# Twelve vector operations on data that nothing reads, in front of the first statistics of a two-layer convolution kernel

## The chip, the cores and the metric

The kernel runs on one core of a Trainium2 chip. A core has a matrix engine (TensorE, PE in the profile), a vector engine (VectorE, DVE), a scalar engine (ScalarE, ACT), a general engine (GpSimd, POOL) and a queue engine that issues transfers (SyncE, SP). Each works through its own queue in order and waits on semaphores for the others. Data lie in a working memory of 128 partitions (SBUF) and in the banks that TensorE writes to (PSUM); 16 DMA engines move data between the device memory and SBUF. The metric is device time in microseconds (us) of one execution; lower is better.

## The reference

The input x has 384 channels of 192 by 192 pixels, float32. Two layers follow each other; both normalise x over 32 groups of 12 channels first (`_gn`: mean and variance over the group's channels and all its pixels) and add their result to x:

```python
x = x + L0(_gn(x), ...)   # 1x1 conv to 3*384 channels, 2x2 max pool, 3x3 depthwise conv,
                          # attention over channels in 8 heads, gelu, repeat, 1x1 conv
x = x + L1(_gn(x), w)     # 7x7 depthwise conv with a symmetrised kernel
```

Nothing of layer 0 can be finished before the group statistics of x are known, since they scale the weights of its first convolution.

## The kernel before, in words

The channels are three tiles of 128 partitions (`KT = 3`), x is cut into 24 blocks of 8 image rows (`NB = 24`, `BLK` = 1536 pixels per channel). The function `conv_preact_d2` builds everything; most of the order on each engine is left to a scheduler, and what is wrapped in `keep` (`tc.keep_in_program_order`) keeps the order in which it is written.

The part around the change, in the order of the text:

- L122 to L151: constants. `ident`, `ones`, `gsel` (which channels share a group) and others are filled by VectorE and POOL.
- L153 to L185: ACT's queue issues the loads of the weights; POOL makes the symmetrised 7x7 weights.
- L253: `vrows, rowbuf`, a buffer for image rows. The change stands right behind this line.
- L255 to L278: the pools `xpool` (three block buffers) and `parkp`; `z`, a tile of ones and zeros, is filled by VectorE (L265, L266), and the PSUM banks `grams`, `bank_x`, `bank_y` and so on are opened.
- L309 to L420: the first statistics, of channel tiles 0 and 1. Pool `xsp`, tag `xs`, has five buffers. The first is taken by `xe` (L317), an extra slice of channel tile 2; the others are cycled through by the blocks. SP issues the loads (L413); VectorE takes `bn_stats` of each 512 pixels (L337, six per block of two channel tiles; L418 for `xe`). The blocks come from the last to the first; 21 go through the five buffers, the last three (b = 2, 1, 0) into buffers of `xpool` that stay (`held`).
- L394 to L408: after 21 blocks the statistics are aggregated (L356) and TensorE sums them over the groups (L344).
- L421 to L434: the three held blocks' statistics are added, mean and reciprocal deviation come out (L377 to L383, with POOL's power), and ACT scales the weights `wq` (L434).
- L436 to L454: TensorE begins the first convolution of the held blocks (L442), ACT sets the sums aside (L448).
- L459 to L482: meanwhile the statistics of channel tile 2 are taken in the same manner (loads L477, tag `xs` again).
- L808: a matrix product on `z` opens the bank `grams`; it is early in TensorE's queue and needs no load.

After that the kernel runs through the first layer, its attention and the second layer, none of which the change touches. A few later lines serve below as examples of what an operation takes: L861 (a 32 by 32 transpose on VectorE of 384 elements per partition), L1269 (a sum over `lower` with its two dimensions swapped, so that it is read with a stride of 24 floats), L1254 (the same sum read densely), L1253 and L1117 (dense vector operations of two inputs), L1510 (an addition that moves pixels in a strided order), L929 (a multiply-add on rows of 96), L233 and L1955 (copies out of PSUM).

Of the kernel before, what the change touches and what calls it, by code (L numbers as in the profile page):

```python
# [8 lines left out]
F32 = mybir.dt.float32  # L9
AF = mybir.ActivationFunctionType  # L10
ALU = mybir.AluOpType
AX = mybir.AxisListType

P = 128
# [72 lines left out]
def conv_preact_d2(  # L87
# [17 lines left out]
    nc = tc.nc  # L105
    PSUM = bass.MemoryType.PSUM
# [17 lines left out]
    ones = const.tile([P, P], F32, name="ones")  # L124
# [119 lines left out]
    def row_tiles(pool, name, n):  # L244

        t = pool.tile([P, n * KT * ROW], F32, name=name)
        rows = [
            t[:, k * ROW : (k + 1) * ROW].rearrange("p (t c) -> p t c", c=PS + 2)
            for k in range(n * KT)
        ]  # L250
        return [rows[k : k + KT] for k in range(0, n * KT, KT)], t

    vrows, rowbuf = row_tiles(rowp, "rows", 3)  # L253

    xctx = ExitStack()  # L255
    xpool = xctx.enter_context(tc.tile_pool(name="xpool", bufs=NX))
    parkp = xctx.enter_context(tc.tile_pool(name="parkp", bufs=1))
# [51 lines left out]
    with tc.tile_pool(name="stp", bufs=1) as stp, tc.tile_pool(name="xsp", bufs=5) as xsp:  # L309
# [57 lines left out]
        def both(kt, most, mid):  # L367

            last = moments(aggregate(kt, 0, NX, "last"), mid, f"{kt}_last")
            nc.vector.scalar_tensor_tensor(most, last, NX / NB, most, ALU.mult, ALU.add)  # L370
            return most
# [107 lines left out]
        d = both(kt, dm, mid)  # L479
# [24 lines left out]
    for i in range(3):  # L504
        w = wq[:, TWO, i * C : (i + 1) * C]
# [926 lines left out]
    for i in range(3):  # L1432
        t = sxp.tile([P, LEAD + CP * RB * RUN + LEAD], F32, name=f"sx{i}")
# [582 lines left out]
```

## Time and profile before

| | us |
|---|---|
| median of 4 runs | 2700.42 (2699.68 to 2701.9) |
| the profiled execution | 2701.9 |
| its span, first to last instruction | 2700.2 |
| TensorE matmul busy | 2506.2 (93%) |
| VectorE busy | 2238.1 (83%) |
| ACT busy | 1420.3 (53%) |
| POOL busy | 1460.3 (54%) |

In the page, the busy times are of the whole span; the view in order of time gives start, length, engine, source line, operation, output and inputs with their shapes (partitions by elements), a count where equal operations follow each other, and in brackets how long the engine had been idle before and what released it. A length includes the time that an instruction overlaps the next one of its engine. "PEld" are TensorE's weight loads. A view by stretch gives, for each engine, the busy time and in brackets the number of instructions, and then the granted TensorE clock, the busy share of the DMA engines and the rate in GB/s.

### The profile page before, as it was taken

How to read it: one execution, taken by the hardware profiler on the slowest of the kernel's cores; microseconds unless marked ns; L12 is line 12 of the kernel's file. 1: busy time of each engine (PE TensorE's matmuls, PEld its weight loads, DVE VectorE, ACT ScalarE, POOL GpSimd, SP SyncE). 2: the span in 40 equal slices, each digit the busy share in tenths (PEclk: the TensorE clock that was granted, in tenths of full speed). 3: DMA queues.
4: the chain of work that ended last, by engine and by line, in shares of the span. 5: the costliest groups of instructions: out<-in, count | busy, mean ns of one | idle time of the engine just before them, and what ended most of it. 6: DMA issues, size and time to landing. Idle time of an engine off the chain costs nothing. (4 is left out here: it accounts for less than half of the span.)

```text
span 2700.2 us, 29574 instructions
## 1 busy us (share of the span) xinstructions
PE 2506.2 (93%) x8893; PEld 1630.7 (60%) x8893; DVE 2238.1 (83%) x3172; ACT 1420.3 (53%) x2711; POOL 1460.3 (54%) x1587
## 2 busy tenths in 40 slices
PE   0298999999999999999899989999999799999998
PEld 0144566656666656665556656666666577777776
DVE  7986788888888888877799969998888789886876
ACT  0032667676767676776212223223234677777776
POOL 1013788888887988875213311001011677777877
PEclk9999999999999999999999989999999899999999
DMA  9962354445453635443429996757657999999998
GB/s 378 400 242 53 109 172 125 148 128 177 118 183 87 190 110 188 112 115 72 141 96 335 373 317 221 241 178 251 211 162 254 328 345 362 368 368 369 371 372 259
DMA packets 467630, 609.59 MB, mean 226 GB/s; under 512 B 250224, under 2 KB 399312, under 8 KB 450704
## 3 DMA queue, kind: packets, MB, share of 16 engines
q1 hardware_dynamic: 407104, 311.83, 36.9%
q0 software_dynamic: 37344, 148.84, 15.5%
q10 hardware_dynamic: 23024, 147.05, 14.6%
q8 instruction: 71, 1.16, 0.2%
q14 instruction: 87, 0.71, 0.1%
HBM read 370.93 MB, written 208.21 MB: 214 GB/s over the span
## 5 line engine op out<-in xcount | busy, mean ns | idle before, releaser
L563 PE MATMUL pv<-xv,wq 128*128 128x384 f32 x1512 | 499.8, 492 | 21.9 <-DMA xv<-in_x_dram 11.0
L1920 PE MATMUL pc<-main,w 128*128 128x288 f32 x1536 | 435.2, 406 | 3.9 <-POOL aux L1848 1.9
L563 PEld LDWEIGHTS pv<-xv,wq 128*128 128x128 f32 x1512 | 290.5, 193 | 222.8 <-issue 10.8
L1940 DVE TENSOR_SCALAR apart<-pc,rb 32x576 f32<-32x576 f32 x384 | 312.2, 813 | 107.3 <-PE pc L1920 98.1
L897 POOL TENSOR_TENSOR qk<-qk,more 128x384 f32<-128x384 f32 x290 | 309.5, 1073 | 110.3 <-ACT more L896 101.4
L1938 ACT ACTIVATE apart<-pc,rb 32x576 f32<-32x576 f32 x384 | 281.0, 732 | 132.5 <-PE pc L1920 127.7
L1551 POOL DMA_DIRECT2D sd<-sx x96 | 72.4, 758 | 506.4 <-DVE sx L1510 487.8
L1920 PEld LDWEIGHTS pc<-main,w 128*128 128x128 f32 x1536 | 290.1, 189 | 87.7 <-PE pc L1920 3.4
L596 DVE SCALAR_TENSOR_TENSOR vb<-rows,wd,vb 128x576 f32<-128x576 f32 x360 | 293.7, 818 | 10.7
L897 POOL TENSOR_TENSOR qk<-qk,rows 128x384 f32<-128x384 f32 x216 | 230.3, 1071 | 76.3 <-ACT rows L896 70.1
L1920 PE MATMUL pc<-aux,h 128*128 128x288 f32 x768 | 248.8, 406 | 0.4 <-POOL main L1828 0.2
L1879 POOL COPY res<-apart 128x1152 f32<-128x1152 f32 (+1 forms) x96 | 218.9, 2311 | 55.0 <-DMA out_dram<-res 42.7
L929 DVE SCALAR_TENSOR_TENSOR bank_r<-ring,wd,bank_r 128x384 f32<-128x384 f32 x383 | 236.3, 617 | 6.9
L1037 PE MATMUL bank_b<-rows,more 128*128 128x384 f32 x528 | 220.6, 500 | 1.9 <-ACT bank_c L1139 1.0
L1510 DVE TENSOR_TENSOR sx<-xr,y 128x576 f32<-128x576 f32 x180 | 203.8, 1173 | 18.8 <-ACT y L1481 15.1
L569 DVE TENSOR_REDUCE rows<-pv 128x192 f32<-128x768 f32 x144 | 137.7, 956 | 59.4 <-PE pv L563 59.3
L1530 ACT ACTIVATE wq<-sx,negmid 128x1152 f32<-128x1152 f32 x96 | 120.6, 1256 | 118.8 <-DVE sx L1510 116.6
L1117 DVE TENSOR_TENSOR rows<-bank_c,rows 128x384 f32<-128x384 f32 x132 | 73.3, 555 | 127.2 <-PE bank_c L1037 68.9
L1920 PEld LDWEIGHTS pc<-aux,h 128*128 128x128 f32 x768 | 144.9, 189 | 43.0 <-POOL main L1828 2.5
L896 ACT ACTIVATE more<-ring,wd 128x384 f32<-128x384 f32 x290 | 170.3, 609 | 0.0
L1456 ACT ACTIVATE gl<-po 128x288 f32<-128x288 f32 x96 | 39.4, 410 | 221.4 <-PE po L1449 221.4
L1037 PE MATMUL bank_x<-xq,wq 128*128 128x384 f32 x378 | 154.8, 491 | 1.0 <-ACT bank_b L1089 1.0
(349 smaller groups left out, 4922.9 us busy)
## 6 DMA issues: line engine op xcount, KB each, us to landing
sd<-sx POOLq DMA_DIRECT2D x96, 600.0 KB, 10.1
out_dram<-res SPq DMA_DIRECT2D x192, 288.0 KB, 11.2
main<-sd ACTq DMA_DIRECT2D x46, 1200.0 KB, 6.6
xr<-in_x_dram SPq DMA_DIRECT2D x45, 1152.0 KB, 12.6
xq<-in_x_dram SPq DMA_DIRECT2D x21, 2304.0 KB, 8.6
xv<-in_x_dram SPq DMA_DIRECT2D x126, 384.0 KB, 8.0
w<-wt ACTq DMA_DIRECT2D x46, 1024.0 KB, 7.5
xs<-in_x_dram SPq DMA_DIRECT2D x24, 1536.0 KB, 15.2
```

What stands on the lines that cost most here:

```text
L563: nc.tensor.matmul(ps[:, u, 0 : RB * HW], wq[:, kt, o : o + P], xb[:, u, kt, :], start=(kt == 0), stop=(kt == KT - 1),)
L569: nc.vector.tensor_reduce(rows[ct][:, 1 + t0 : 1 + t0 + UT, 1 : PS + 1], ps[:, :, 0 : RB * HW].rearrange("p u (a w b) -> p u w a b", a=2, ...
L596: pin(nc.vector.scalar_tensor_tensor(dst, src, w, dst, ALU.mult, ALU.add))
L896: keep(nc.scalar.mul(part.rearrange("p (h w) -> p h w", w=PS), src, w))
L897: keep(nc.gpsimd.tensor_tensor(flat, flat, part, ALU.add))
L929: nc.vector.scalar_tensor_tensor(into, src, w, before, ALU.mult, ALU.add)
L1037: nc.tensor.matmul(ps[:, 0:HN], lhs, rhs, start=start, stop=True, skip_group_check=True)
L1510: nc.vector.tensor_tensor(bass.AP(flat.tensor, flat.offset + at(e) + a * RUN, [flat.ap[0], [JP, NT], [1, NJ], [at(f) - at(e), 2]],), xq[:, ...
L1879: keep(copy(res[ps, k], apart[ps, :, k].rearrange("p e n -> p n e")))
L1920: nc.tensor.matmul(ahead[q][:, k, 0 : NT * NJ], lhs, rhs, start=(j == 0), stop=(j == 2), skip_group_check=True,)
L1938: keep(nc.scalar.mul(dst, src, scale))
L1940: keep(nc.vector.tensor_scalar_mul(dst, src, scale))
```

## The change

Two SBUF tiles of 6144 floats per partition (`tin`, `tout`) and two PSUM banks (`bank`) are opened for a while and closed again before `xpool` opens. VectorE fills all three with ones, does seven transposes of 768 elements per partition with different strides, an addition of 256 elements with strides and one scaled copy of 288 elements out of PSUM; ACT does two more of these copies. Nothing reads `tout` afterwards. All of it is pinned in the order of the text among itself. Since the space is used again by what is opened next, TensorE's L808 and the load of the first held block now wait for ACT's copies. Lines behind L253 move down by 34; the line numbers in the text are those of the kernel before.

```diff
     vrows, rowbuf = row_tiles(rowp, "rows", 3)
 
+    with tc.tile_pool(name="trial", bufs=1) as trial, tc.tile_pool(
+        name="trial_p", bufs=1, space=PSUM
+    ) as trial_p:
+        order_of = tc.keep_in_program_order
+        tin = trial.tile([P, 6144], F32, name="tin")
+        tout = trial.tile([P, 6144], F32, name="tout")
+        bank = trial_p.tile([P, 2, 512], F32, name="trial_b")
+        order_of(nc.vector.memset(tin, 1.0))
+        order_of(nc.vector.memset(bank, 1.0))
+        order_of(nc.vector.memset(tout, 1.0))
+
+        def v(t, *dims):
+            return bass.AP(t.tensor, t.offset, [t.ap[0], *[list(d) for d in dims]])
+
+        def w(t, o, *dims):
+            return bass.AP(t.tensor, t.offset + o, [t.ap[0], *[list(d) for d in dims]])
+
+        turn = lambda a, b: order_of(nc.vector.transpose(a, b))
+        turn(v(tout, (1, 768)), v(tin, (1, 768)))
+        turn(v(tout, (32, 24), (1, 32)), v(tin, (1, 24), (24, 32)))
+        turn(v(tout, (8, 24), (192, 4), (1, 8)), v(tin, (32, 24), (1, 32)))
+        turn(w(tout, 576, (8, 24), (-192, 4), (1, 8)), v(tin, (32, 24), (1, 32)))
+        turn(v(tout, (8, 24), (192, 4), (1, 8)), v(tin, (384, 12), (32, 2), (1, 32)))
+        turn(v(tout, (1, 24), (24, 32)), v(tin, (32, 24), (1, 32)))
+        turn(v(tout, (192, 4), (8, 24), (1, 8)), v(tin, (32, 24), (1, 32)))
+        order_of(nc.vector.tensor_tensor(
+            w(tout, 2048, (68, 2), (8, 32), (1, 4)), w(tout, 2048, (68, 2), (8, 32), (1, 4)),
+            v(tin, (32, 2), (0, 4), (1, 32)), ALU.add))
+        order_of(nc.vector.tensor_scalar_mul(
+            v(tout, (1, 2), (32, 12), (384, 12)), v(bank, (512, 2), (12, 12), (1, 12)), tin[:, 0:1]))
+        order_of(nc.scalar.mul(
+            w(tout, 1, (1, 2), (32, 12), (384, 12)), v(bank, (512, 2), (12, 12), (1, 12)), ones[:, 0:1]))
+        order_of(nc.scalar.mul(
+            w(tout, 2048, (12, 2), (24, 12), (1, 12)), v(bank, (512, 2), (12, 12), (1, 12)), ones[:, 0:1]))
     xctx = ExitStack()
```

In an access pattern each pair is a stride and a count in floats, the outermost first.

## The prediction

> **What bounds the kernel now.** I read the page first, then the order in time at the start of the run, since the change stands there.
>
> ```profile
> span 2700.2 us, 29574 instructions
> ...
> PE 2506.2 (93%) x8893; PEld 1630.7 (60%) x8893; DVE 2238.1 (83%) x3172; ACT 1420.3 (53%) x2711; POOL 1460.3 (54%) x1587
> ```
>
> TensorE carries the kernel as a whole, but it has nothing to do before the first statistics are in. VectorE in order of time (start, length, instruction, count; in brackets the idle time before it and what ended it):
>
> ```profile
> 1.46 0.48 DVE L266 MEMSET z<- 128x512 f32 x1
> 7.17 2.86 DVE L418 BATCH_NORM_STATS2 ste<-xe 128x6 f32<-128x384 f32 x6 [5.22 <-DMA xe<-in_x_dram]
> ...
> 10.41 0.15 DVE L420 TENSOR_SCALAR me<-mve 128x1 f32<-128x1 f32 x1
> 13.98 3.66 DVE L337 BATCH_NORM_STATS2 st<-xs 128x6 f32<-128x512 f32 x6 [3.42 <-DMA xs<-in_x_dram]
> 18.20 3.66 DVE L337 BATCH_NORM_STATS2 st<-xs 128x6 f32<-128x512 f32 x6 [0.56 <-DMA xs<-in_x_dram]
> 26.38 3.66 DVE L337 BATCH_NORM_STATS2 st<-xs 128x6 f32<-128x512 f32 x6 [4.52 <-DMA xs<-in_x_dram]
> 30.29 68.01 DVE L337 BATCH_NORM_STATS2 st<-xs 128x6 f32<-128x512 f32 x108 [0.25 <-DMA xs<-in_x_dram]
> 98.22 3.56 DVE L356 BATCH_NORM_AGGREGATE mv_most<-st 128x2 f32<-128x378 f32 x2
> ...
> 105.56 10.77 DVE L337 BATCH_NORM_STATS2 st<-xs 128x6 f32<-128x512 f32 x18
> ...
> 120.42 37.47 DVE L337 BATCH_NORM_STATS2 st<-xt 128x6 f32<-128x512 f32 x63
> ```
>
> Two things are to be seen. First, idle time until 26.38: VectorE starts waiting at 1.95 and waits for loads in four pieces, 5.22 + 3.42 + 0.56 + 4.52 = 13.7 us. Second, a small reserve in the long stretch: 108 statistics take 98.22 - 30.29 = 67.93 us, 0.629 each, while 18 of them on data long landed take (10.77 - 0.68) / 17 = 0.594 each. So from 30.29 on a block of six comes every 3.77 us, where VectorE alone needs 3.58; the loads set that pace. 18 blocks hold 67.93 - 18 x 3.58 = 3.5 us that a late VectorE can win back. After 98.22 it can win back nothing: the 18 and the 63 run at 0.594, without waits.
>
> That stretch releases TensorE (all engines in order of time, then a stretch by engine):
>
> ```profile
> 120.45 1.12 POOL L382 TENSOR_TENSOR rstd<-rstd,halfneg 128x1 f32<-128x1 f32 x2 [88.48 <-DVE mean L383]
> 121.07 2.77 ACT L434 ACTIVATE wq<-wq,rstd 128x768 f32<-128x768 f32 x4 [100.57 <-POOL rstd L382]
> 122.06 6.30 PE L442 MATMUL bank_b<-xs,wq 128*128 128x512 f32 x8 [2.16 <-ACT wq L434]
> ...
> 140.00:160.00 20.00, 20.00 (x48) 8.80 (x47) 20.00 (x33) 7.02 (x12) 0.00 (x0) 1.00 0.95 357
> ```
>
> From 122 TensorE is full (20.00 of 20.00 us) and VectorE too, so what is late at 98.22 ends the kernel that much later.
>
> **The prices.** From the views by tile and by line (shortest, middle and longest ns; start; shape):
>
> ```profile
> L265 DVE MEMSET z<- x1: 308/308/308, 1.1 to 1.1; 128x300 f32 x1
> L266 DVE MEMSET z<- x1: 485/485/485, 1.5 to 1.5; 128x512 f32 x1
> ...
> L861 DVE STREAM_TRANSPOSE turns<-qk x144: 534/578/579, 203.3 to 1297.3; 128x384 f32<-128x384 f32 x144
> ...
> L1269 DVE TENSOR_REDUCE after<-lower x1: 1575/1575/1575, 1322.2 to 1322.2; 128x24 f32<-128x576 f32 x1
> ...
> L1254 DVE TENSOR_REDUCE seconds<-sq x3: 753/753/754, 1325.7 to 1352.1; 128x24 f32<-128x576 f32 x3
> ```
>
> - Memset: 177 ns for 212 elements, 0.835 ns each; 6144 elements are 5.13 us from start to start. Two of them: 10.26.
> - Memset of the two PSUM banks, 1024 elements: no row has one. Below, the same slope, 0.86 us; above, the slope of VectorE's copies out of PSUM (L1955 282 ns for 128, L233 558 for 384: 1.08 ns), 1.10. I take 0.95, nearer to the memset rows.
> - Dense transpose of 768: 578 + 384 x 1.04 (the slope of the statistics, 543 ns for 384, 676 for 512) = 978 ns; the statistics start 83 ns before their predecessor's recorded end (676 long, 593 apart), so 0.89 from start to start. Four more of the seven are like it for VectorE: the third to fifth write runs of 8, the seventh's pattern folds into a contiguous one. No row has runs of 8 in a store, so their upper bound is the next price.
> - The second transpose reads with a stride of 24 floats. L1269 reduces along the same stride, L1254 the same shape densely: 822 ns more for 576 elements, 1.43 ns each, 1.10 us for 768. So 1.99. The sixth stores with that stride: between nothing more and the same 1.10, middle 0.55, so 1.44; no row speaks for either end.
> - The strided sum of 256: L1253 takes 458 ns for 288 densely, so 0.35 apart. The scaled copy of 288 out of PSUM: 0.38 by the copies above, up to 0.41 more for scattered stores; I take 0.58.
>
> Memset against a rule: the Trainium skill, "VectorE: DVE Perf Modes", section "Zero memsets can be issued as uint32 (trn2)", says that a memset takes one cycle per element whatever its type, and the same page gives VectorE 0.96 GHz. That is 6.40 us for 6144, against 5.13 by the rows; by the rule both memsets would cost 2.5 us more and the forecast would be 2704.8. The rows are of the same instruction on the same memory, so I go by them.
>
> **The change, step by step.** In the built program VectorE's queue has 12 new operations, ACT's two; the order on all engines is otherwise the old one but for one thing: the new operations are interleaved with the first xs block's statistics, and xe's six statistics stand behind them. VectorE after:
> - 1.10 + 5.13 + 0.95 + 5.13 = 12.31; z 0.26, first transpose 0.89, z 0.43, second 1.99: 15.88. The first xs block (landed at 13.98) waits 1.9 us.
> - Its six statistics 3.58; transposes three, four, five and seven 3.56; the sixth 1.44; the sum 0.35; the copy 0.58: 25.39. The transposes wait for one another's end, but a statistic stands between each two, which covers the wait; without it each would lose its 0.08 of overlap, 0.4 in all.
> - xe's statistics 6 x 0.463 = 2.78: 28.17. Second block 3.58 and the small ones 0.40: 32.15. Third block: 35.73.
>
> The fourth block began at 30.29, so VectorE is 5.4 us late there. Of the 20.0 us of new work, 14.6 disappear in the old waits: the 13.7 above, 0.25 at 30.29 and small gaps. 18 blocks win back 3.5; 1.9 are left at 98.22 and reach the end.
>
> Loads: tag xs has five buffers, xe holds one. The fifth xs load waits for xe's statistics and goes out at 28.2 instead of 19.7; the third and fourth are then still in flight (landing at 26.38 and 30.29), and xe's own load took 6.3 us from issue to landing, so it lands by 34.5 instead of 34.06, where VectorE wants it only at 39.3. Later loads are issued up to 5.4 us later of a lead whose middle was 15.2. Were that cover gone, each late load would cost what it lands late.
>
> Costs at nothing: ACT's two copies (under 1 us each at about 26) end in its idle stretch of 100.57 us; ACT's queue only needs to be free at 121. The first matmul of TensorE (L808) now waits for ACT's reading of the bank, 2.0 becomes about 27; behind it in the queue stands L344 at 100.2. The held loads wait for ACT too, but go out at 79.8. POOL's queue is unchanged.
>
> Sum: the profiled execution took 2701.9 (1.7 around the span), 1.5 over the median of the four runs; 2701.9 + 1.9 = 2703.8 for it, and from the median 2700.4 **2702.3**.
>
> **The rivals.**
> - *All hidden.* If strides cost nothing (1.10, 0.55 and 0.20 less), 1.9 shrinks to 0.1: 2700.5. For it: the loads set the pace until 98. Against: L1269.
> - *Slower.* Stores in runs of 8 are scattered for VectorE too: transposes three to five cost 1.99 each, the sixth too. 3 x 1.10 + 0.55 = 3.85 more, 5.8 in all, 2706.2. It decides from 2.0 us per transpose on. For it: L1510, which moves pairs with strides, takes 1174 ns for 576 where dense L1253 takes 757. Against: runs of 96 cost little (L929 617 ns for 384, dense L1117 558), and 8 lies between 2 and 96.
> - *Faster.* No wait is removed; only another order of loads could do it.
> - *The work isn't done*, since nothing reads it: then 2700.4. Against it, all twelve operations stand in VectorE's queue. 0.00.
>
> **How the numbers follow.** 0.2% (5.4 us) is about what a measurement of this kernel can tell from no change. Likeliest case 0.60, own range 2700.9 to 2703.8 (sixth transpose, copy and bank at their ends: 0.9 more or 0.8 less; the scatter of the runs: 0.6). All hidden 0.22. In between 0.05: the three transposes with runs of 8 dearer than dense, but not by 1.10 each. Slower 0.11: runs of 8 dear. Faster 0.02. The first three stay within 0.2%: 0.87. The range takes in the hidden case with the scatter of the runs (2699.7 to 2701.9) and reaches to the edge of the slower one: 2699.8 to 2706.0.
>
> **What would show it.** Right: memsets of about 5.1 us, the first block's statistics between 16 and 25, no waits for loads between 26 and 90, the aggregates at about 100.1, TensorE's L442 at about 124. Wrong: transposes three to five near 2 us; or L442 still at 122; or waits for loads behind a late VectorE, which would mean that the late releases starve the queue; or a gap that opens after 122.

## The result, and the profile after

| | us |
|---|---|
| before, median of 76 runs | 2701.28 (2694.54 to 2711.72) |
| after, median of 51 runs | 2706.89 (2696.9 to 2720.32) |
| ratio after / before, 95% interval | 1.0018 (1.0012 to 1.0025) |
| the profiled execution after (span) | 2704.29 (2702.6) |

The ratio is estimated from the runs and is not the quotient of the two medians, which would be 1.0021 (5.6 us). By the ratio the change costs 4.9 us (3.2 to 6.8). The forecast was 2702.3 from a median of 2700.42, so 1.9 us; the measured time lies 0.9 us above the range. Line numbers of the kernel after are 34 higher from L254 on.

The first two lines of the page after:

```profile
span 2702.6 us, 29590 instructions
...
PE 2507.0 (93%) x8893; PEld 1632.7 (60%) x8893; DVE 2260.3 (84%) x3184; ACT 1421.3 (53%) x2713; POOL 1465.2 (54%) x1587
```

VectorE has twelve instructions more (3184 against 3172) and 22.2 us more of busy time; the span of this one execution is only 2.4 us longer. Where most of the work went is seen in VectorE's order of time at the start (start, length, instruction, count; in brackets the idle time before and what ended it):

```profile
2.32 5.18 DVE L262 MEMSET tin<- 128x6144 f32 x1 [1.23 <-issue]
7.71 0.91 DVE L263 MEMSET trial_b<- 128x1024 f32 x1 [0.21 <-issue]
9.89 5.18 DVE L264 MEMSET tout<- 128x6144 f32 x1 [1.27 <-issue]
15.08 0.31 DVE L299 MEMSET z<- 128x300 f32 x1
15.42 0.98 DVE L272 STREAM_TRANSPOSE tout<-tin 128x768 f32<-128x768 f32 x1
...
16.86 1.89 DVE L272 STREAM_TRANSPOSE tout<-tin 128x768 f32<-128x768 f32 x1
18.68 0.65 DVE L371 BATCH_NORM_STATS2 st<-xs 128x6 f32<-128x512 f32 x1
19.26 0.95 DVE L272 STREAM_TRANSPOSE tout<-tin 128x768 f32<-128x768 f32 x1
...
23.61 2.06 DVE L272 STREAM_TRANSPOSE tout<-tin 128x768 f32<-128x768 f32 x1
...
28.45 2.83 DVE L452 BATCH_NORM_STATS2 ste<-xe 128x6 f32<-128x384 f32 x6
...
38.55 3.65 DVE L371 BATCH_NORM_STATS2 st<-xs 128x6 f32<-128x512 f32 x6
...
89.57 13.14 DVE L371 BATCH_NORM_STATS2 st<-xs 128x6 f32<-128x512 f32 x22
102.63 3.56 DVE L390 BATCH_NORM_AGGREGATE mv_most<-st 128x2 f32<-128x378 f32 x2
```

The row at 38.55 is the fourth block (30.29 before). Every wait for a load is gone, as expected. But the memsets do not lie end to end in their rows: 1.23, 0.21 and 1.27 us of "issue" stand ahead of them. From the end of one to the end of the next, the last one takes 9.89 + 5.18 - (7.71 + 0.91) = 6.45 us, not 5.13. The view of VectorE's waits between 0 and 95 us (what waited, for what; us in total, times, longest) has nothing else left:

```profile
DVE tout L264 <- issue: 1.3, 1, 1.3
DVE tin L262 <- issue: 1.2, 1, 1.2
DVE ones L125 <- PEq L2035: 0.9, 1, 0.9
DVE trial_b L263 <- issue: 0.2, 1, 0.2
```

A stretch of the kernel after (length; busy time and instructions of PE, PEld, DVE, ACT, POOL; granted clock, busy share of the DMA engines, GB/s) shows the paced part:

```profile
32.00:100.00 68.00, 0.00 (x0) 0.00 (x0) 68.00 (x117) 0.00 (x0) 0.17 (x1) 1.00 1.01 413
```

VectorE is busy for 68.00 of 68.00 us and is itself the bound now; the loads still run at 413 GB/s. And the release of TensorE, all engines in order of time:

```profile
124.87 1.12 POOL L416 TENSOR_TENSOR rstd<-rstd,halfneg 128x1 f32<-128x1 f32 x2 [92.70 <-DVE mean L417]
125.49 2.77 ACT L468 ACTIVATE wq<-wq,rstd 128x768 f32<-128x768 f32 x4 [95.57 <-POOL rstd L416]
126.47 2.93 PE L476 MATMUL bank_b<-xs,wq 128*128 128x512 f32 x3 [2.16 <-ACT wq L468]
```

The aggregate starts at 102.63 instead of 98.22, TensorE's first matmul of the layer (L442, now L476) at 126.47 instead of 122.06: 4.41 us late both times, with nothing lost or won between.

The two profiled executions alone do not show these 4.41 us at the end. Compared matmul by matmul, the kernel after is 3.9 us behind at 1300 us, 3.1 at 1900, 0.4 at 2500, and its span ends 2.4 us later. Single executions wander by several us there (see the part on the scatter), so what arrives at the end is read from the many runs: 4.9 us, with 4.4 inside the interval.

So the account by the two traces is: VectorE got 23.0 us of new work (14.0 for the memsets end to end, 9.0 for the rest from start to start); 18.6 of them went into waits and into the reserve of the paced blocks, and 4.4 came out at the aggregate.

### The profile page after: what moved, and what is told of

It is laid out like the page before. It is cut to its first block, busy times and chain, and to the rows that moved or that the text cites. A ratio compares the mean times of both kernels' runs of the same rounds, so it can differ in the third digit from the quotient of the medians.

```text
span 2702.6 us, 29590 instructions
## 1 busy us (share of the span) xinstructions
PE 2507.0 (93%) x8893; PEld 1632.7 (60%) x8893; DVE 2260.3 (84%) x3184; ACT 1421.3 (53%) x2713; POOL 1465.2 (54%) x1587
## 4 chain that ended last, share of the span: by engine, by line
PE 73%; DMA 13%; DVE 9%; POOL 2%; issue 2%; SPq 1%; ACT 1%; POOLq 0%; DVEq 0%; ACTq 0%
PE pv L597 19%; DMA out_dram<-res 11%; PE bank_b L1071 9%; PE pc L1954 7%; PE bank_y L1071 6%; PE bank_d L1071 6%; PE bank_c L1071 6%; PE bank_x L1071 6%; PE pr L1507 4%; DVE st L371 3%; PE po L1483 3%; PE grams L830 2%; DVE sx L1544 1%; POOL res L1913 1%; DVE vb L630 1%
```

## The experiments

Two theories were set against each other. **Theory A**: the twelve operations are work in front of a stage with a fixed amount of cover; what exceeds the cover comes out at the aggregate and reaches the end one to one, and the memsets, at 1.04 ns per element, are why it is 4.4 and not 1.9. **The rivals**: the loss is in proportion to the work, or it has a price of its own that cover does not touch (late loads, the pinned order, the waits of TensorE and ACT). All kernels of one group ran on the same chip beside the kernel before.

### Short memsets, and the memsets alone

The first run keeps the change and fills only what the later operations read (768 + 640 elements of `tin` and 384 of `tout`; the expectation says 1536 for the first two):

```diff
-        order_of(nc.vector.memset(tin, 1.0))
+        order_of(nc.vector.memset(tin[:, 0:768], 1.0))
+        order_of(nc.vector.memset(tin[:, 768:4608].rearrange("p (n c) -> p n c", c=384)[:, :, 0:64], 1.0))
         order_of(nc.vector.memset(bank, 1.0))
-        order_of(nc.vector.memset(tout, 1.0))
+        order_of(nc.vector.memset(tout[:, 2048:2432], 1.0))
```

> Theory A: the changed kernel loses its time because VectorE is 4.4 us late at the first aggregate, and half of that lateness is the memsets, which hold VectorE 1.042 ns per element (end to end 6.41 us for 6144) although their rows are 0.835 ns per element long. Here only the elements that are read are filled (1536 and 384 in place of twice 6144), everything else of the change stays. By A VectorE has 24.1 us of work before the third block, which lands at 26.4, so it is not late: aggregate at 98.2 to 98.5, ratio to the kernel before 1.000. Rival B: the loss comes from the strided transposes, the PSUM copies or the waits for ACT; then most of the 1.0018 stays, aggregate later than 101.

The second keeps the three memsets of the change and drops what follows them (the transposes, the sum and the three copies):

```diff
         order_of(nc.vector.memset(bank, 1.0))
         order_of(nc.vector.memset(tout, 1.0))
-        turn = lambda a, b: order_of(nc.vector.transpose(a, b))
-        ...
```

> Only the three memsets of the change, without transposes, sum and copies. Theory A: the memsets end at 15.1, z at 15.9, first block, extra slice and second block at 26.3; the third block lands at 26.4, so VectorE is in time: aggregate at 98.2 to 98.6, ratio 1.000. Together with the run with short memsets this says that each half is free and only both together cost 4.4 us. Rival C: what is added in front costs about in proportion to its length, memsets 13.9 of 22.8 us: 2.7 us, ratio 1.001, aggregate at about 101.

Measured: the short memsets took 2710.96 us against 2711.27 of the kernel before, ratio 1.0005 (0.9994 to 1.0016); the memsets alone 2712.68, ratio 1.0004 (0.9992 to 1.0016). The aggregates start at 98.33 and 98.20 us (98.22 before). VectorE in order of time, with the short memsets:

```profile
14.08 0.69 DVE L372 BATCH_NORM_STATS2 st<-xs 128x6 f32<-128x512 f32 x1 [0.35 <-DMA xs<-in_x_dram]
...
26.50 3.66 DVE L372 BATCH_NORM_STATS2 st<-xs 128x6 f32<-128x512 f32 x6 [1.75 <-DMA xs<-in_x_dram]
30.41 30.13 DVE L372 BATCH_NORM_STATS2 st<-xs 128x6 f32<-128x512 f32 x48 [0.25 <-DMA xs<-in_x_dram]
...
98.33 3.56 DVE L391 BATCH_NORM_AGGREGATE mv_most<-st 128x2 f32<-128x378 f32 x2
```

and with the memsets alone:

```profile
26.34 3.66 DVE L348 BATCH_NORM_STATS2 st<-xs 128x6 f32<-128x512 f32 x6 [0.17 <-DMA xs<-in_x_dram]
30.26 30.14 DVE L348 BATCH_NORM_STATS2 st<-xs 128x6 f32<-128x512 f32 x48 [0.27 <-DMA xs<-in_x_dram]
...
98.20 3.56 DVE L367 BATCH_NORM_AGGREGATE mv_most<-st 128x2 f32<-128x378 f32 x2
```

Each half still waits for the third and fourth block, so each is wholly hidden: 0.1 and 0.0 us at the aggregate. Together they cost 4.41. At the aggregate the loss isn't in proportion to the work, and it isn't a price of the transposes, of the pinned order or of the waits for ACT, which the first of the two runs keeps; it is what is left when the cover is used up. The end times could not have told this: both intervals reach to 1.0016, which is 4.3 us.

### More of the same work

```diff
         order_of(nc.vector.memset(tout, 1.0))
+        for t in (tin, tout, tin, tout):
+            order_of(nc.vector.memset(t, 1.0))
```

> The changed kernel with four more memsets of 6144. Nothing covers them any more, so by theory A (6.41 us each) the aggregate comes 25.6 us later than in the changed kernel, at 128.3, and the time is 4.4 + 25.6 = 30.0 us over the kernel before, ratio 1.0111. If the rows' length (5.18 us) were what they cost and the 1.25 us in front of each a delay of the first instructions alone: 20.7 more, aggregate at 123.3, 25.1 us over before, ratio 1.0093. If the later part of the kernel gave lateness back, as the end of the changed kernel's profile looks like, less than the aggregate's shift would arrive at the end.

Measured: 2742.9 us against 2711.27, ratio 1.0121 (1.01 to 1.0142), that is 32.8 us (27.1 to 38.5). The aggregate starts at 128.26, TensorE's first matmul 30.03 us later than before. The memsets in order of time:

```profile
9.89 5.18 DVE L264 MEMSET tout<- 128x6144 f32 x1 [1.27 <-issue]
16.30 5.18 DVE L266 MEMSET tin<- 128x6144 f32 x1 [1.23 <-issue]
22.70 5.18 DVE L266 MEMSET tout<- 128x6144 f32 x1 [1.23 <-issue]
...
128.26 1.84 DVE L392 BATCH_NORM_AGGREGATE mv_most<-st 128x2 f32<-128x378 f32 x1
```

They start 6.41 us apart, and 4.41 + 4 x 6.41 = 30.05. With the cover gone, each memset comes out in full, at 6.41 and not at its row's 5.18, and the kernel's end follows: 30.0 lies inside the interval of the 32.8. This is the run that decides the price of a memset: with the rows' price the aggregate would stand at 123.3.

### A sweep of sizes and strides

Memsets of 768 to 6144 elements, and transposes of 768 elements with load strides 1, 2, 3, 4, 8, store strides 2, 3, 4, 8 and stores in runs of 2 and 4, in place of what the change does after its first two memsets:

```diff
+        for n in (768, 1536, 3072, 6144):
+            order_of(nc.vector.memset(tout[:, 0:n], 1.0))
+        turn = lambda a, b: order_of(nc.vector.transpose(a, b))
+        dense = lambda t: v(t, (32, 24), (1, 32))
+        for k in (1, 2, 3, 4, 8):
+            turn(dense(tout), v(tin, (32 * k, 24), (k, 32)))
+        for k in (2, 3, 4, 8):
+            turn(v(tout, (32 * k, 24), (k, 32)), dense(tin))
+        for k in (2, 4):
+            turn(v(tout, (k, 24), (192, 32 // k), (1, k)), dense(tin))
```

> Prices by themselves: memsets of 6144, 1024 (PSUM), 768, 1536, 3072 and 6144, then transposes of 768 whose loads have strides of 1, 2, 3, 4 and 8 floats, whose stores have strides of 2, 3, 4 and 8, and whose stores come in runs of 2 and 4. Theory A: each memset holds VectorE 1.042 ns per element whatever its size, in rows of 0.70, 1.34, 2.62 and 5.18 us. Transposes: if what counts is how many neighbours lie in the same 16 bytes (the Trainium skill, SBUF - State Buffer, on cachelines), strides of 2 and runs of 2 cost the dense 0.95 us, strides of 4 and 8 the 1.9 us that stride 24 took, 3 in between. If the distance counts, cost grows with the stride and 2 already costs more. The whole is some 11 us more work than the change's: aggregate at 112 to 116.

Measured in one execution: the aggregate starts at 111.20 us, a little under what was expected. VectorE in order of time; the transposes shown are load strides 3, 4 and 8, then store strides 4 and 8 and runs of 4:

```profile
12.52 2.62 DVE L265 MEMSET tout<- 128x3072 f32 x1 [0.59 <-DVE z L289]
...
17.10 5.18 DVE L265 MEMSET tout<- 128x6144 f32 x1 [1.23 <-issue]
...
25.64 1.19 DVE L270 STREAM_TRANSPOSE tout<-tin 128x768 f32<-128x768 f32 x1
...
27.31 1.53 DVE L270 STREAM_TRANSPOSE tout<-tin 128x768 f32<-128x768 f32 x1
...
29.32 1.55 DVE L270 STREAM_TRANSPOSE tout<-tin 128x768 f32<-128x768 f32 x1
...
34.03 1.51 DVE L270 STREAM_TRANSPOSE tout<-tin 128x768 f32<-128x768 f32 x1
...
35.80 1.55 DVE L270 STREAM_TRANSPOSE tout<-tin 128x768 f32<-128x768 f32 x1
...
38.92 0.97 DVE L270 STREAM_TRANSPOSE tout<-tin 128x768 f32<-128x768 f32 x1
```

The rows of the memsets grow by (5.18 - 2.62) / 3072 = 0.833 ns per element, and the idle time ahead of them grows too, by (1.23 - 0.59) / 3072 = 0.208 ns; together 1.041 ns. So a fifth of a memset is booked as a gap in front of its row (the 0.59 is even put down to another memset, `z`). Of the transposes, stride 2 costs nothing in a load (0.956 us), 3 costs 0.24 us more than dense, 4 and 8 cost 0.58 and 0.60, stores nearly the same, and runs of 2 and 4 in the store are dense (0.967 and 0.970). So 2 is free and 3 lies between, as expected, but 4 and 8 take 1.5 us and not the 1.9 of stride 24.

### The change once more, and the loads in another order

If the cover is made of waits for loads, taking waits out of the kernel before must make the change dearer. A part of the waits was put down to `wq` (1728 KB, L162), which ACT's queue sends for at the very start, ahead of most of the blocks. A first attempt moves that load behind ACT's small loads, without and with the change; the change itself ran beside them.

```diff
-    nc.scalar.dma_start(wq, wqkvT.rearrange("(t p) o -> p t o", p=P))
     nc.scalar.dma_start(bq, bqkv)
     ...
+    nc.scalar.dma_start(wq, wqkvT.rearrange("(t p) o -> p t o", p=P))
```

> The kernel before with one move: the load of wq (1.7 MB) is issued behind ACT's small loads instead of ahead of them. In the kernel before SP's third xs load waits 11.2 us for the small load bp, which stands behind wq, and the DMA engines run at 126 and 187 GB/s from 16 to 22. Theory A says that what the first aggregate gains the end gains: third block 4 us earlier, aggregate at 94 to 95, L442 at 118, ratio 0.9985. Rival: wq's bytes only come later among the blocks, the aggregate stays at 98, ratio 1.000.

> The change and the move of wq together. By theory A the changed kernel has VectorE busy from 1.1 to 102.6 without a wait for a load, so earlier loads can't help it: aggregate again at 102.6, L442 at 126.5, ratio to the kernel before 1.0016; the price of the change against the kernel with small loads first is then 8 us and not 4.4. If the price were that of the work itself, the aggregate would come at about 98.5.

> The changed kernel once more, beside the two below on one chip. Theory A: TensorE's first product on x (L442) at 126.5 instead of 122.1, 4.4 us, and the ratio near 1.0016; what differs from that in one execution comes from TensorE's wait for loads between 1550 and 1610, which was 11 us in the profile of before, 25 in that with the memsets alone.

Measured against 2713.11 us of the kernel before on that chip: 2712.39 with the load moved, ratio 0.9995 (0.9983 to 1.0006); 2714.23 with the change on top, 1.0002 (0.9992 to 1.0012); the change alone 2716.18, 1.0011 (1.0 to 1.0023). The aggregates start at 98.50, 102.62 and 102.63. VectorE in order of time, with the load moved:

```profile
14.44 3.66 DVE L337 BATCH_NORM_STATS2 st<-xs 128x6 f32<-128x512 f32 x6 [4.85 <-DMA xs<-in_x_dram]
...
23.54 3.66 DVE L337 BATCH_NORM_STATS2 st<-xs 128x6 f32<-128x512 f32 x6 [1.45 <-DMA xs<-in_x_dram]
30.36 3.66 DVE L337 BATCH_NORM_STATS2 st<-xs 128x6 f32<-128x512 f32 x6 [3.16 <-DMA xs<-in_x_dram]
```

The attempt missed its aim: the waits only moved from the third block to the fourth, since `wq` still travels ahead of the aggregate, and the first block's load now goes out at 6.2 us instead of 1.3. The kernel without the change got no faster, so these runs can't tell a price of cover from a price of its own. What they repeat is the change's 4.1 and 4.4 us at the aggregate. At the end, the run with both misses its expectation: 1.0016 lies above its interval, although its first matmul (L476) starts at 126.46, as late as with the change alone. Where its profile loses the lateness again stands in the part on the scatter.

The second attempt takes `wq` out of the stage: SP sends for it behind the last held block.

```diff
-    nc.scalar.dma_start(wq, wqkvT.rearrange("(t p) o -> p t o", p=P))
...
             nc.sync.dma_start(xb, xv[:, 0:TWO, b * BLK : (b + 1) * BLK])
+            if b == 0:
+                nc.sync.dma_start(wq, wqkvT.rearrange("(t p) o -> p t o", p=P))
```

> The kernel before, with wq's load (1.7 MB, needed by ACT only at 121) taken out of ACT's queue and issued by SP behind the last held block. The run with the small loads first gained nothing because wq's bytes still went out ahead of the first aggregate and the first block's load was issued 4.9 us later. Here 4.2 us of transfer (1.77 MB at 417 GB/s) leave the stretch ahead of the aggregate: first block at about 11.5, one block each 3.77, aggregate at 90 to 93, L442 at 114 to 117. Theory A (what is gained at the aggregate reaches the end): 5 to 8 us, ratio 0.997 to 0.998. Rival: the loads that follow or a later stage take it back, ratio 1.000 although the aggregate is early.

> The same with the change. Theory A: VectorE works from 1.1 on without a wait for a load, so its aggregate stays at 102.6 and L442 at 126.5; the same twelve operations then cost 10 to 12 us against the kernel with wq behind the blocks, where they cost 4.4 against the kernel before. Ratio to the kernel before 1.0016, and 1.004 to the kernel with wq behind the blocks. If the work had a price of its own, the aggregate would come 4.4 us behind that of the other run, at 95 to 97.

Measured against 2711.48 us: without the change 2707.79, ratio 0.9991 (0.9979 to 1.0002); with it 2717.64, ratio 1.0021 (1.0009 to 1.0034). VectorE in order of time without the change:

```profile
18.63 3.66 DVE L336 BATCH_NORM_STATS2 st<-xs 128x6 f32<-128x512 f32 x6 [0.32 <-DMA xs<-in_x_dram]
22.59 37.72 DVE L336 BATCH_NORM_STATS2 st<-xs 128x6 f32<-128x512 f32 x60 [0.30 <-DMA xs<-in_x_dram]
...
94.34 3.56 DVE L355 BATCH_NORM_AGGREGATE mv_most<-st 128x2 f32<-128x378 f32 x2
```

and with it:

```profile
102.61 3.59 DVE L389 BATCH_NORM_AGGREGATE mv_most<-st 128x2 f32<-128x378 f32 x2
```

Without the change the 4.52 us wait is gone and the aggregate starts 3.88 us earlier (less than the 5 to 8 expected; 1728 KB at the 416 GB/s of that stage are 4.25 us, about what was won). With the change the aggregate stands at 102.61, where it stands without the moved load too. The twelve operations now cost 102.61 - 94.34 = 8.27 us against the kernel that has `wq` late, and (1.0021 - 0.9991) x 2711.5 = 8.1 us at the end. The two profiled executions, on one chip, are 8.31 us apart at TensorE's first matmul (118.18 and 126.49) and 8.5 us in their spans (2704.4 and 2712.9), so here the lateness can be followed to the end. But the pair is not as clean as it was meant to be: with the change the scheduler let SP send for `wq` at 8.8 us already (77.5 without the change), so its bytes were in the stage after all, and a price of its own of 4.4 us on the old supply would give 102.6 as well. What speaks in this run is that VectorE had no wait for a load up to 95 us, so that no other supply could have helped it; the case against a price of its own rests on the two halves that cost nothing.

Without the change this last kernel has the lowest ratio of all, with a median 3.7 us under the kernel before, but its interval just reaches 1, so a gain is likely and not shown.

### Where the scatter of the runs sits

The medians of the kernel before differ by chip (2701 in the first runs, 2711 to 2713 in those of the experiments). In the profiles one stretch of the second layer carries much of such differences, at about 1560 us, where TensorE waits for the load of `xv`. The columns are those of the stretches above; the kernel before in its first profile:

```profile
1560.00:1575.00 15.00, 4.12 (x6) 1.56 (x7) 3.66 (x4) 4.42 (x10) 6.33 (x9) 0.64 1.04 368
```

and the kernel with the memsets alone:

```profile
1560.00:1575.00 15.00, 0.00 (x0) 0.00 (x0) 4.48 (x4) 3.18 (x7) 5.08 (x7) 0.62 1.03 374
```

TensorE's longest wait there was 5.3 us in the first and 18.6 us in the second (all its waits there 11.0 and 23.2 us; the expectation above has 25). The changed kernel had 5.1 us in its first profile and 17.5 us when run again on another chip; it was 18.7 with `wq` behind the blocks and the change. The DMA engines are full in all of them (1.03, 1.04). So it goes with the chip or the execution, not with the edit. What makes the one stretch short and the other long was not followed up.

A second such stretch is at about 1330 us. With the change and the small loads first, TensorE is 4.3 us behind the kernel before at 1300 us, matmul by matmul, and 1.1 us at 1334; in between, its idle time ahead of a matmul on `xv` is 2.72 us, against 4.50 in the change run again, and its clock was granted in full (first the change run again, then the small loads first with the change):

```profile
1325.00:1340.00 15.00, 10.50 (x28) 5.65 (x27) 12.90 (x18) 4.50 (x18) 1.10 (x2) 0.89 0.87 290
1325.00:1340.00 15.00, 12.28 (x38) 6.87 (x37) 14.03 (x19) 4.50 (x18) 0.59 (x1) 1.00 0.86 289
```

This is one execution, and whether the moved loads or chance did it stays open.

## Why the prediction was wrong, point by point

**The mechanism held.** VectorE's late start was to be covered by its four waits first, then by the reserve of the paced blocks, and what was left was to reach the end one to one. The first two are shown, and the third as far as TensorE's first matmul: no wait for a load is left up to 95 us, the blocks won back 38.55 - 30.29 = 8.26 down to 4.41, 3.85 against the 3.5 forecast, and the 4.41 stand unchanged there. At the end the ratios of the change (4.9 us, 3.2 to 6.8) and of the four memsets more (32.8 us, 27.1 to 38.5) agree with it; the run with the small loads first and the change does not. The runs with half the work and with four memsets more moved the aggregate as this says (0 and 30 us).

**The step that failed is the price of the memsets**: "Memset: 177 ns for 212 elements, 0.835 ns each; 6144 elements are 5.13 us from start to start". 0.835 is the slope of the row's length, and it was taken for the spacing of the rows. Measured, each of the two takes 6.41 to 6.45 us end to end, 1.04 ns per element, and the one on PSUM 1.12, just over its upper bound of 1.10: together 2.8 us more. The prediction's own sign, "memsets of about 5.1 us", came true in the rows (5.18) and said nothing of the price; "the aggregates at about 100.1" and "TensorE's L442 at about 124" showed it wrong (102.63 and 126.47). The same two rows of the kernel before would have told it, read by their ends: 1.46 + 0.48 = 1.94 and 1.10 + 0.31 = 1.41 lie 0.53 apart, and the first ends some 0.33 after its predecessor (1.02 + 0.06 = 1.08), so 0.20 to 0.22 for 212 elements, about 1 ns each. The page's two decimals blur it (the raw times give 0.541 - 0.320 = 0.221, 1.04 ns), but not down to 0.835.

**The rule weighed was right.** The Trainium skill, "VectorE: DVE Perf Modes", section "Zero memsets can be issued as uint32 (trn2)", gives one cycle per element. With the page's 0.96 GHz that is an estimate of 1.042 ns; measured 1.041. The prediction said what the sum would be by it, 2704.8, and 2700.4 + 4.41 is 2704.8. That the two agree to a tenth is partly luck: VectorE came to the fourth block 0.3 us later than by that sum, and the paced blocks won back 0.35 more than forecast. "The rows are of the same instruction on the same memory, so I go by them" was true of the rows and wrong of how they were read: a row that disagrees with a rule by a fifth calls for a second reading of the same trace, by the ends, before it is preferred.

**The smaller terms**, from start to start: the sixth transpose 1.85 against 1.44, so a store with a stride of 24 floats lies nearer to its upper bound of 1.99 than to the middle that was taken (+0.41); the second 1.82 against 1.99; the dense ones 0.88 against 0.89; the sum 0.31 against 0.35; the copy out of PSUM 0.55 against 0.58. The statistics of `xe` and the two blocks behind them took 0.2 less. All in all VectorE reached the fourth block at 38.55 instead of 35.73, 2.82 late, of which the memsets are 2.77.

**The rivals.** *Slower* by dear stores in runs of 8 fell: transposes three to five have rows of 0.95 like the dense ones (0.98). *All hidden* fell, since strides of 24 do cost (1.89 and 2.06). *Costs at nothing* held for ACT (two copies, 0.75 and 0.50 us, at 28.6 and 29.4), for L808 (30.0 instead of 2.0, the next thing in its queue far behind) and for the loads, since nobody waits for one. But they went otherwise than forecast: the fifth goes out at 27.9 when the first block's statistics end, not those of `xe`, and the next four go out 8 to 13 us late, not up to 5.4; these four land 0.9 to 1.5 us later than before, 5.6 to 7.0 us ahead of a VectorE that is late itself.

**The range** was too narrow above because the memset had one value and no bound: two prices that differed by 2.5 us stood side by side in the text, and only one entered the range. The median of before, 0.9 us higher over 76 runs than over the four, adds to it. With the price by the rule and that median the sum would be 2705.7, inside the range; the last 1.2 us, by which the medians lie further apart than 4.4, no trace places; 5.6 us lies inside the ratio's interval. By the ratio the change is slower by 0.18%; the interval, 0.12% to 0.25%, lies on both sides of the 0.2% that the prediction named as the limit of what can be told from no change.

## What to carry to other kernels

Price an operation by the distance from the end of its predecessor to its own end, over two sizes, and not by the length of its row: part of it can be booked as a gap ahead of it. Before adding work in front of a stage, add up the cover there (waits, then the reserve of a paced loop). In this kernel, work up to that sum was free, and beyond it every microsecond came out at the aggregate, so two edits that are free one by one can cost together. And where a rule and a row disagree, keep both as ends of the range.

## What the runs showed of the hardware beside this

- An "issue" gap is not always idle time. Ahead of memsets it grows with the memset that follows: 0.15 us for 768 elements, 0.59 for 3072, 1.23 for 6144.
- Transposes of 768 elements on VectorE by the distance between the elements of a load: 0.95 us at 1, 0.96 at 2, 1.19 at 3, 1.53 at 4, 1.55 at 8, and 1.89 at 24 in the change; stores 0.98, 1.19, 1.51, 1.55 at 2, 3, 4, 8 and 2.06 at 24. The Trainium skill, "SBUF — State Buffer", section "Specifications (TRN2)", has lines of 16 bytes and wants two hits in a line: strides of 2 and of 4 floats, on the two sides of it, agree. That 24 is dearer than 8 by 0.34 and 0.51 us is not explained by it, and no run here looked into it; the two also differ in the range they walk over (768 floats with 24, 6144 with 8).
